# Attention by seven products, followed by a cluster block and an MLP: a ninth score before the first block, the maxima row copied one unit earlier, and x brought back by adding DMA transfers

## The chip, the cores and the metric

The kernel runs on one core of one Trainium2 chip. The metric is the device time of the kernel in microseconds (us), a median over several runs. All data are float32.

Names used below: PE is TensorE (matmuls; PEld its weight loads), DVE is VectorE, ACT is ScalarE, POOL is GpSimd, SP is SyncE, which here only issues DMAs. Each engine has its own queue of instructions and works through it in order.

## The reference

Two layers are applied to x of shape (4, 256, 64, 64), that is, four images of 256 channels and N = 4096 pixels. The first is full self-attention over the pixels:

```python
q = jnp.einsum('oc,bcn->bno', wq, xf) + bq          # 32 channels
k = jnp.einsum('oc,bcn->bon', wk, xf) + bk[None, :, None]
attn = jax.nn.softmax(jnp.einsum('bnd,bdm->bnm', q, k), axis=-1)   # 4096 x 4096
v = jnp.einsum('oc,bcn->bon', wv, xf) + bv[None, :, None]
out = jnp.einsum('bcn,bmn->bcm', v, attn).reshape(B, C, H, W)
return gamma[0] * out + x
```

The second is a block of three parts. A group norm over the whole image, then a clustering of the pixels (features and values by 1x1 convolutions, 4 heads of 24 channels, centres from average pooling, every pixel given to the most similar centre), a projection, and a residual:

```python
y = x + ls1[...] * cluster(group_norm(x, gn1_w, gn1_b), f_w, f_b, v_w, v_b, proj_w, proj_b, sim_alpha, sim_beta)
hdn = conv1x1(group_norm(y, gn2_w, gn2_b), mlp_w1, mlp_b1)      # 256 -> 1024
hdn = conv1x1(jax.nn.gelu(hdn), mlp_w2, mlp_b2)                 # 1024 -> 256
y = y + ls2[...] * hdn
z = jax.nn.relu(batch_norm(y * dw_w[...], dw_g, dw_b, dw_m, dw_v))
z = jax.nn.relu(batch_norm(conv1x1(z, pw_w), pw_g, pw_b, pw_m, pw_v))
```

The first group norm needs mean and variance of the attention's result over all channels and pixels of an image, so nothing of the cluster block can start before the last pixel of the attention is done.

## The kernel before, in words

The four images are worked on one after the other: attention, cluster, MLP. The beginning of the next image's attention (projections, and its first eight scores) is put between the instructions of the cluster and the MLP of the image before it. For image 0 a prologue, `alone`, does it.

**Units.** The attention of an image is a loop of 64 units: 8 blocks `nb` of 512 query pixels, by 8 groups `g` of 512 key pixels. A unit u = 8 nb + g has an SBUF slot of 128 x 2048 numbers (`slots[u]`), in which its scores, then their exponentials lie. There are 12 slots, two of them in the space of the MLP's weights.

**Scores.** A score is made in two halves (`half`). A half is two matmuls into a PSUM tile `sc` (L409), a copy to the slot by ACT (`kept`, L422), and a maximum against the block's running maximum `top` by DVE (L434; L437 for the first of a block, which compares the second half in PSUM with the copied first half). The tile pool `ps_s` has two PSUM buffers; the loop keeps one of them all the time as `hold`, so all scores use the other one, and the next half's matmuls wait for the maximum of the half before.

**Maximum of a query.** After the last score of a block, `fold` and `highest` reduce `top` over partitions to a row of 512 maxima. The row goes through DRAM and comes back spread over all partitions in SBUF (`mr`), and `known` (L531, ACT) copies it into `hold` in PSUM. `highest` is a generator of three steps: a transpose and a reduction on DVE, four small copies on ACT, a reduction, a transpose and the two DMAs. For block 0 the row is made on chip (`across`, `spread`).

**Exponentials.** `exps(u)` subtracts the row from the slot in two DVE instructions (L547), then ACT takes three exponentials (L550, L551, L554) or, in the plain unit g=7, two (L553, L554). `factors(u)` forms with one DVE instruction (L577) and four on POOL (L557) the sums that the seven-product scheme multiplies, and adds to the sum of the exponentials `acc`.

**Weighting.** `weigh(u, av, part)` multiplies values and exponentials in four parts. Units g=0 to 6 use seven products in place of eight on 2 x 2 quarters (28 matmuls, L640), unit g=7 the plain form (18 matmuls, L618).

**Order of a unit.** The order is written out by hand in the loop of `weighting`: the score halves of part 0; `gather` and `known` at g=7; `clear`, which takes the seven-product sums out of PSUM; `exps(u+1)`; maxima; work for the block before; weigh part 0; score halves of part 1; weigh part 1; halves of part 2; `factors(u+1)`; weigh part 2; halves of part 3; weigh part 3; then `tail(u)`. Which half of which score p goes where is set by the table `at`, made by `due_at`: in quarters of a unit, score p (counted from the first that is left to the loop) is due at (14i+10)/5 and (14i+17)/5 for images 1 to 3, at 3i+2 and (6i+7)/2 for image 0; a second bound keeps a score at most LEAD = 11 units ahead, and from p=16 on no earlier than unit 6.

**End of a block.** `clear` and `complete` (L680, DVE) turn the products in PSUM into the attention's numerator `t`; `total` makes the row of denominators, `leave` multiplies by their reciprocals (POOL), `sent` writes the block to DRAM (`att`).

**x comes back.** The group norm's statistics need gamma x attention + x + bias. In the last ten units `load(i)` reads x again from DRAM in four tiles of 1024 pixels (SP's queue), `back(i)` reads the attention of three of them (`tb`, 1 MB each, SP's queue), and `add(i)` puts both and the bias `gbv` together on DVE (L726). The last tile's two blocks are added from SBUF by `add_one` (L726 too). `seen(nb)` (bn_stats, L743) and `pooled(nb)` (L748) take the statistics of a block on DVE.

**At the ends.** `derived` computes constants from the parameters: two square roots on ACT (L193; square root and exponential need different tables in ACT), small DVE instructions and three transposes or matmuls for a weight. It is called as `early` at the end of unit 1 of image 0. At the end of an MLP the next image's `first`, `exps(0)` and `factors(0)` stand ahead of the last pointwise part (`last`).

Of the kernel before, what the change touches and what calls it, by code (L numbers as in the profile page):

```python
# [8 lines left out]
F32 = mybir.dt.float32  # L9
# [5 lines left out]
P = 128  # L15
B, C, H, W = 4, 256, 64, 64
N = H * W
KC = C // P
# [35 lines left out]
def attention_then_cluster_block(  # L54
# [167 lines left out]

    def derived():

        for s, e, g, v, m, b_ in (
            (dw_d, dw_e, "dw_g", "dw_v", "dw_m", "dw_b"),
            (pw_s, pw_e, "pw_g", "pw_v", "pw_m", "pw_b"),
        ):
            rsqrt(s, par(v), BN_EPS)
# [12 lines left out]
        tps = ps_s.tile([P, 2, NB], F32, tag="s", name="wf_p")[:, 0]  # L242
# [5 lines left out]
        nc.vector.tensor_copy(wf_t, tps[:ED, :C])  # L248
        nc.vector.tensor_copy(fvb[:, :ED], tps[:, C : C + ED])
# [43 lines left out]
    def attention(b, xs, ys):  # L293
# [129 lines left out]

        def half(u, h):
# [8 lines left out]
            if g:  # L433
                return lambda: nc.vector.tensor_tensor(top, sc, top, ALU.max)  # L434
            if h:
                first = slots[u][:, PAIR[0]].rearrange("p h r n -> p r h n")
                return lambda: nc.vector.tensor_tensor(tiles(top), tiles(sc), first, ALU.max)  # L437
# [121 lines left out]
        def factors(u):  # L559
# [8 lines left out]
            if g >= SEVEN:  # L568
                if g == SEVEN:
                    plus(both, both, one, ALU.subtract)  # L570
                for acc, q in ((both, B11), (one, B12), (both, B21), (one, B22)):
                    plus(acc, acc, s[:, q])
# [82 lines left out]
        def clear(nb, av):  # L655
# [9 lines left out]
            plus(t[:, 1], t[:, 1], t[:, 0], ALU.subtract)  # L665
            plus(t[:, 3], t[:, 1], t[:, 3], ALU.subtract)
            plus(t[:, 1], t[:, 1], t[:, 2])
            plus(t[:, 2], t[:, 2], t[:, 3])
# [50 lines left out]

        def back(i):  # L720

            t = own["back", i] = spool.tile([P, KC, XT], F32, tag="s", name=f"tb_{b}_{i}")
            nc.sync.dma_start(out=t, in_=own["t"][i].rearrange("p k b n -> p k (b n)"))

        def join(y, t, k):
            nc.vector.scalar_tensor_tensor(y, y, gbv[:, k : k + 1], t, ALU.add, ALU.add)  # L726

        def add(i):

            t = own.pop(("back", i))  # L730
            for k in range(KC):
                join(ys[i][:, k], t[:, k], k)

        def add_one(nb):

            t = ts.pop(nb)
            for k in range(KC):
                y = block(ys, k, nb).rearrange("p (h n) -> p h n", h=2)
                join(y, rows_of(t, k), k)
# [18 lines left out]
        def alone():  # L758
# [13 lines left out]
            for u in range(GRP):  # L772
# [7 lines left out]
                if u % 2 and 4 + u // 2 < SEVEN:  # L780
                    for f in sums(4 + u // 2):
                        f()
                if u == 3:
                    load_rest()
            fold(0)
# [1157 lines left out]
```

## Time and profile before

| | us |
|---|---|
| median of 3 runs | 3443.86 (3443.59 to 3446.1) |
| profiled execution | 3447.51 |
| its span | 3445.7 |
| weighting loop of image 0 | 82.6 to 612.5 |
| image 1 | 938.8 to 1458.6 |
| image 2 | 1785.4 to 2305.1 |
| image 3 | 2607.6 to 3126.3 |
| one matmul of 128x512, mean (L409) | 0.478 |
| copy of a half (L422) | 1.010 |
| maximum of a half (L434) | 1.221 |

The profile is of one execution; a row of the groups gives line, engine, operation, output<-input with the shape, count, then the busy time of all and the mean in ns of one, then the idle time of the engine just before them and what ended it. A row of the waits gives the waiting instruction, what released it, the total, the number of times and the longest. A row of the timeline gives start and duration, and in brackets the idle time before it and its releaser. A row of the stretches gives busy time (and number of instructions) of PE, PEld, DVE, ACT and POOL between two times, the granted clock of PE, and the share and rate of DMA.

### The profile page before, as it was taken

To read this page: it belongs to the slowest core of one execution; us is meant where nothing else is said; L and a number is where in the kernel's file an instruction comes from. 1 tells how busy PE (TensorE), PEld (TensorE's weight loads), DVE (VectorE), ACT (ScalarE), POOL (GpSimd) and SP (SyncE) were. 2 spreads that over 40 slices of the span, in tenths; PEclk is the share of its full clock that TensorE was granted. 3 is DMA by queue.
4 is the path that set the end of the run, shared out by engine and by line. 5 is a ranking of instruction groups with operands and counts; after the bars stand their busy time and mean duration, and the time that the engine had idled before them with its cause. 6 is when DMAs were issued, how large, how long until landed. Compare 5 with 4: busy or idle time off the path is not lost.

```text
span 3445.7 us, 40484 instructions
## 1 busy us (share of the span) xinstructions
PE 3145.7 (91%) x13866; PEld 2484.0 (72%) x13866; DVE 2519.6 (73%) x3666; ACT 1713.1 (50%) x2706; POOL 2234.8 (65%) x2150
## 2 busy tenths in 40 slices
PE   6799998899979999799988999989997899988999
PEld 4577776688657777578866777767875677766687
DVE  4688887677668788766766888776776788876675
ACT  3456562445545655244554555524454565634444
POOL 3467777368447878737835777854763778774664
PEclk8899999999999999899999999989999999999999
DMA  4111214100111111410011111231011111130000
GB/s 152 34 49 56 62 50 154 65 25 28 47 37 59 58 57 53 161 59 19 28 43 37 60 57 59 92 115 59 19 41 39 56 56 62 50 133 1 13 19 25
DMA packets 104062, 197.20 MB, mean 57 GB/s; under 512 B 14672, under 2 KB 29616, under 8 KB 102320
## 3 DMA queue, kind: packets, MB, share of 16 engines
q1 hardware_dynamic: 102896, 193.50, 17.4%
q8 instruction: 110, 1.80, 0.2%
q10 hardware_dynamic: 832, 1.11, 0.1%
q14 instruction: 96, 0.79, 0.1%
q0 software_dynamic: 128, 0.00, 0.0%
HBM read 148.32 MB, written 46.25 MB: 56 GB/s over the span
## 4 chain that ended last, share of the span: by engine, by line
PE 49%; DVE 19%; POOL 15%; issue 9%; ACT 8%; DMA 0%; SPq 0%; ACTq 0%; POOLq 0%; DVEq 0%
PE av L640 10%; PE mo L1559 9%; POOL acc L557 7%; DVE s L547 5%; PE hq L1642 5%; DVE top L434 4%; PE sc L409 4%; DVE t L577 4%; POOL t L557 4%; PE hp L1642 3%; POOL s L557 3%; PE hr L1642 3%; PE fv L1137 3%; PE vp L366 3%; PE av L618 2%
## 5 line engine op out<-in xcount | busy, mean ns | idle before, releaser
L422 ACT COPY s<-sc 128x1024 f32<-128x1024 f32 x512 | 514.0, 1010 | 581.7 <-PE sc L409 567.6
L557 POOL TENSOR_TENSOR s<-t,s 128x512 f32<-128x512 f32 x224 | 285.8, 1276 | 612.8 <-DVE t L577 546.6
L547 DVE TENSOR_TENSOR s<-s,hold 128x1024 f32<-128x1024 f32 x512 | 599.6, 1212 | 71.1 <-ACT hold L531 68.8
L434 DVE TENSOR_TENSOR top<-sc,top 128x1024 f32<-128x1024 f32 x392 | 478.5, 1221 | 155.9 <-ACT s L422 153.0
L409 PE MATMUL sc<-q,k 128*128 128x512 f32 x1024 | 401.0, 478 | 154.9 <-DVE top L434 99.1
L640 PE MATMUL av<-t,v 128*128 128x256 f32 x1792 | 484.1, 394 | 26.8 <-DVE t L680 19.2
L640 PE MATMUL av<-s,v 128*128 128x256 f32 x1792 | 474.8, 388 | 32.2 <-ACT s L551 25.7
L640 PE MATMUL av<-s,sum 128*128 128x256 f32 x1792 | 473.4, 388 | 0.0
L557 POOL TENSOR_TENSOR acc<-acc,t 128x512 f32<-128x512 f32 x352 | 459.2, 1323 | 0.0
L577 DVE TENSOR_TENSOR t<-s,hold 128x1024 f32<-128x1024 f32 x224 | 273.1, 1219 | 198.9 <-ACT s L554 116.3
L640 PEld LDWEIGHTS av<-s,v 128*128 128x128 f32 x1792 | 348.1, 195 | 96.3 <-ACT s L551 29.1
L640 PEld LDWEIGHTS av<-t,v 128*128 128x128 f32 x1792 | 352.2, 198 | 87.0 <-issue 20.7
L1597 ACT ACTIVATE hs<-hs,pv_s 128x256 f32<-128x256 f32 x496 | 232.4, 503 | 344.4 <-DVE hs L1633 344.4
L640 PEld LDWEIGHTS av<-s,sum 128*128 128x128 f32 x1792 | 349.3, 195 | 57.7
L1559 PE MATMUL mo<-hs,w 128*128 128x256 f32 x1512 | 385.3, 381 | 0.4 <-ACT hs L1597 0.4
L409 PEld LDWEIGHTS sc<-q,k 128*128 128x128 f32 x1024 | 177.7, 194 | 265.9 <-DVE top L434 113.4
L557 POOL TENSOR_TENSOR t<-s 128x512 f32<-128x512 f32 x224 | 302.9, 1352 | 34.4 <-PE av L640 16.2
L550 ACT ACTIVATE hold<-s 128x512 f32<-128x512 f32 x224 | 134.8, 602 | 376.6 <-DVE s L547 376.6
L1559 PEld LDWEIGHTS mo<-hs,w 128*128 128x128 f32 x1512 | 283.1, 190 | 47.6 <-ACT hs L1597 6.9
L554 ACT ACTIVATE s<-s 128x1024 f32<-128x1024 f32 x256 | 266.9, 1043 | 0.8
L1633 DVE TENSOR_TENSOR hs<-hq,hs 128x256 f32<-128x256 f32 x496 | 198.6, 421 | 79.6 <-PE hq L1642 69.3
L618 PE MATMUL av<-s,v 128*128 128x512 f32 (+1 forms) x576 | 232.0, 549 | 6.2 <-ACT s L553 6.2
(288 smaller groups left out, 5220.1 us busy)
## 6 DMA issues: line engine op xcount, KB each, us to landing
k<-k SPq DMA_DIRECT2D x256, 256.0 KB, 2.7
x<-in_x SPq DMA_DIRECT2D x62, 512.0 KB, 5.7
out<-xn SPq DMA_DIRECT2D x62, 256.0 KB, 2.1
att<-t SPq DMA_DIRECT2D x48, 256.0 KB, 3.8
tb<-att SPq DMA_DIRECT2D x12, 1024.0 KB, 7.1
q<-q SPq DMA_DIRECT2D x32, 256.0 KB, 4.1
w<-in_w SPq DMA_DIRECT2D x8, 1024.0 KB, 7.8
mr<-row_mx SPq DMA_DIRECT2D x28, 256.0 KB, 3.3
```

The source lines that it names most:

```text
L409: nc.tensor.matmul(sc[:, r, :], k_s[:, (2 * h + r) * P : (2 * h + r + 1) * P], qs[u // GRP], start=True, stop=True,)
L422: nc.scalar.copy(slots[u][:, PAIR[h]].rearrange("p h r n -> p r h n"), tiles(sc))
L434: return lambda: nc.vector.tensor_tensor(top, sc, top, ALU.max)
L547: nc.vector.tensor_tensor(sh, sh, mb.to_broadcast([P, 2, 2, QW]), ALU.subtract)
L554: nc.scalar.activation(s[:, PAIR[1]], s[:, PAIR[1]], AF.Exp)
L557: nc.gpsimd.tensor_tensor(out, x, y, op)
L577: nc.vector.tensor_tensor(t31[u], s[:, B11 : B22 + 1 : 2], b12.to_broadcast([P, 2, 2, QW]), ALU.add)
L618: nc.tensor.matmul(av[2 + c].rearrange("p (h n) -> p h n", h=2)[:, h], own["v"][:, RG * g + t, c * P : (c + 1) * P], s[:, PAIR[t // 2], t ...
L640: nc.tensor.matmul(av[bank][:, half_ * QW : (half_ + 1) * QW], a[:, r], t[:, r], start=(g == 0 and r == 0 and i in (1, 7, 2, 4)), stop=(g ...
L1559: return nc.tensor.matmul(bank[:, half * HB : (half + 1) * HB], a[:, j], t, start=start, stop=stop)
L1597: nc.scalar.activation(src, src, AF.Gelu_apprx_tanh, bias=pvc("b1", P, j + 4 * (i > 1)))
L1642: nc.tensor.matmul(out, w, x, start=True, stop=True)
```

## The change

The change has six parts.

1. The two square roots of `derived` become `roots`, called in the prologue at u=6; the transposes become `wf`, also in the prologue, with a tile of another PSUM pool and copies by ACT. The rest of `derived` is called within unit 0.
2. The ninth score (unit 8) is done ahead of the loop also for images 1 to 3: its first half at the end of the MLP before `exps(0)`, its second after the last pointwise part, `factors(0)` after it.
3. The table of due times is another one, the same for all images: score p, counted from 9, is due at 7i//2 and (14i+7)//4 quarters; LEAD is the only other bound.
4. The first maximum of a block is taken from the two copies in SBUF, not from PSUM. It is held back and issued with the next maximum or at the end of g=5 (`held`, `opened`). For blocks after the first, `known` moves from the start of g=7 to after weigh part 1 of g=6. The second step of `highest` moves from the start of the unit to after `factors`.
5. x is loaded as before, ACT adds the bias (`shift`), and the attention is added to it in SBUF by a DMA with `accum_op=ALU.add` on POOL's queue (`back`, three times, and `back_one` for block 6). `seen` and `pooled` move into the units, one block each.
6. In the last block `clear`, and half of the last sum of exponentials, move from POOL to DVE, and `complete(nb, av, 0)` is called after weigh part 1 of g=7.

```diff
+    def roots():
+        for s, v in ((dw_d, "dw_v"), (pw_s, "pw_v")):
+            rsqrt(s, par(v), BN_EPS)
+        table(AF.Exp)
+
     def derived():
...
-            rsqrt(s, par(v), BN_EPS)
...
-        tps = ps_s.tile([P, 2, NB], F32, tag="s", name="wf_p")[:, 0]
+    def wf():
+
+        tps = ps_m.tile([P, NB], F32, tag="m", name="wf_p")
...
-        nc.vector.tensor_copy(wf_t, tps[:ED, :C])
-        nc.vector.tensor_copy(fvb[:, :ED], tps[:, C : C + ED])
+        nc.scalar.copy(wf_t, tps[:ED, :C])
+        nc.scalar.copy(fvb[:, :ED], tps[:, C : C + ED])
...
+        held = []
+
+        def opened():
+            while held:
+                held.pop()()
...
             if g:
-                return lambda: nc.vector.tensor_tensor(top, sc, top, ALU.max)
+
+                def against():
+                    opened()
+                    nc.vector.tensor_tensor(top, sc, top, ALU.max)
+
+                return against
             if h:
-                first = slots[u][:, PAIR[0]].rearrange("p h r n -> p r h n")
-                return lambda: nc.vector.tensor_tensor(tiles(top), tiles(sc), first, ALU.max)
+
+                a, z = (slots[u][:, q].rearrange("p h r n -> p r h n") for q in PAIR)
+                held.append(lambda: nc.vector.tensor_tensor(tiles(top), a, z, ALU.max))
...
                 for acc, q in ((both, B11), (one, B12), (both, B21), (one, B22)):
-                    plus(acc, acc, s[:, q])
+                    eng = nc.vector if acc is one and nb == NBLK - 1 else nc.gpsimd
+                    eng.tensor_tensor(acc, acc, s[:, q], ALU.add)
...
+        def shift(i):
+            for k in range(KC):
+                nc.scalar.activation(
+                    ys[i][:, k], ys[i][:, k], AF.Identity, bias=gbv[:, k : k + 1]
+                )
+
         def back(i):
 
-            t = own["back", i] = spool.tile([P, KC, XT], F32, tag="s", name=f"tb_{b}_{i}")
-            nc.sync.dma_start(out=t, in_=own["t"][i].rearrange("p k b n -> p k (b n)"))
-
-        def join(y, t, k):
-            nc.vector.scalar_tensor_tensor(y, y, gbv[:, k : k + 1], t, ALU.add, ALU.add)
...
+            nc.gpsimd.dma_start(
+                out=ys[i], in_=own["t"][i].rearrange("p k b n -> p k (b n)"), accum_op=ALU.add
+            )
+
+        def back_one(nb):
+            nc.gpsimd.dma_start(
+                out=block_all(nb), in_=own["t"][nb // 2][:, :, nb % 2], accum_op=ALU.add
+            )
...
+                if u == 6:
+                    roots()
             fold(0)
+            for g in range(4, SEVEN):
+                for f in sums(g):
+                    f()
             dgs["dg"] = across(0)
+            half(GRP, 0)
             spread(0, dgs["dg"])
+            wf()
+            half(GRP, 1)
             exps(0)
             factors(0)
-            score(GRP)
...
-        for p in range(GRP + (b == 0), units):
-            i = p - GRP - (b == 0)
-            q = ((14 * i + 10) // 5, (14 * i + 17) // 5) if b else (3 * i + 2, (6 * i + 7) // 2)
+        for p in range(GRP + 1, units):
+            i = p - GRP - 1
+            q = (7 * i // 2, (14 * i + 7) // 4)
             for h in range(2):
-                at_least = max(RG * (p - LEAD), RG * 6 if p >= 2 * GRP else 0) + 2 * h
-                due_at(*divmod(max(q[h], at_least), RG), p, h)
+                due_at(*divmod(max(q[h], RG * (p - LEAD) + 2 * h), RG), p, h)
...
+            views = {units - 8 + i: i for i in range(6)} | {units - 1: 6}
+
             def tail(u):
...
-                    (units - 11, lambda: (load(0), back(0))),
-                    (units - 10, lambda: load(1)),
-                    (units - 9, lambda: (add(0), back(1), load(2))),
-                    (units - 8, lambda: (seen(0), pooled(0), seen(1), load(3))),
-                    (units - 7, lambda: (pooled(1), add(1), back(2))),
-                    (units - 6, lambda: (seen(2), pooled(2))),
-                    (units - 5, lambda: (seen(3), pooled(3), add(2), next_x(), next_x())),
-                    (units - 4, lambda: (seen(4), pooled(4), load_mix(b), next_x())),
+                    (units - 11, lambda: load(0)),
+                    (units - 10, lambda: (load(1), shift(0), back(0))),
+                    (units - 9, lambda: (load(2), shift(1), back(1))),
+                    (units - 8, lambda: (load(3), shift(2), back(2))),
+                    (units - 7, lambda: shift(3)),
+                    (units - 5, lambda: (next_x(), next_x())),
+                    (units - 4, lambda: (load_mix(b), next_x())),
                     (units - 4, lambda: b == B - 1 and load_mlp(b)),
-                    (units - 3, lambda: (seen(5), pooled(5), add_one(6), next_x(), begin())),
-                    (units - 2, lambda: (seen(6), pooled(6), b < B - 1 and load_mlp(b))),
+                    (units - 3, lambda: (next_x(), begin())),
+                    (units - 2, lambda: (back_one(6), b < B - 1 and load_mlp(b))),
...
-                    if more:
+                    if more and nb == 0:
                         known(mb)
                 if g == SEVEN:
-                    clear(nb, av)
+                    clear(nb, av, nc.gpsimd if more else nc.vector)
...
                     peak = highest(nb + 1)
                     next(peak)
-                    next(peak)
+                if u == 0:
+                    early()
+                if u in views:
+                    seen(views[u])
                 weigh(u, av, 0)
                 for f in due(u, 1):
                     f()
                 weigh(u, av, 1)
+                if g == GRP - 1 and not more:
+                    complete(nb, av, 0)
+                if more and nb and g == GRP - 2:
+                    known(mb)
                 maxima = due(u, 2)
                 if g + 1 < GRP or more:
                     factors(u + 1)
                 if ripe:
+                    next(peak)
                     mb = next(peak)
                 for f in maxima:
                     f()
+                if u in views:
+                    pooled(views[u])
                 weigh(u, av, 2)
                 for f in due(u, 3):
                     f()
+                if g == 5:
+                    opened()
...
-                elif nb and g == 5 and nb < NBLK - 1:
+                elif nb and g == 5:
                     sent(nb - 1)
                 weigh(u, av, 3)
-                if u == 1:
-                    early()
...
-                if g == GRP - 1:
+                if g == GRP - 1 and more:
                     complete(nb, av, 0)
...
         finish(blocks - 1, acc)
-        if nxt:
-            nxt.exps(0)
-            nxt.factors(0)
-        last(blocks - 1, False, nc.vector)
...
+        if nxt:
+            nxt.half(GRP, 0)
+            nxt.exps(0)
+        last(blocks - 1, bool(nxt), nc.vector)
+        if nxt:
+            nxt.half(GRP, 1)
+            nxt.factors(0)
```

## The prediction

> **What bounds the kernel now.** I read the page's head and groups first, then the waits, then the weighting loop by stretches and unit by unit.
>
> ```profile
> span 3445.7 us, 40484 instructions
> PE 3145.7 (91%) x13866; PEld 2484.0 (72%) x13866; DVE 2519.6 (73%) x3666; ACT 1713.1 (50%) x2706; POOL 2234.8 (65%) x2150
> L434 DVE TENSOR_TENSOR top<-sc,top 128x1024 f32<-128x1024 f32 x392 | 478.5, 1221 | 155.9 <-ACT s L422 153.0
> L409 PE MATMUL sc<-q,k 128*128 128x512 f32 x1024 | 401.0, 478 | 154.9 <-DVE top L434 99.1
> ```
>
> PE is nearly always at work, and what it still waits for is mostly one thing: the single free PSUM buffer of the scores. A half score is L409, then the ACT copy L422 (1.01 us), then the DVE maximum L434 (1.22 us), and only then may the next L409 start: about 3.3 us per half at best (3.09 from start to start at 954.46 and 957.55). The waits name who gives the buffer back, and one more cause:
>
> ```profile
> PEld sc L409 <- DVE top L434: 113.4, 205, 4.8
> DVE s L547 <- ACT hold L531: 68.8, 27, 3.7
> PE sc L409 <- DVE top L437: 32.0, 27, 4.9
> ```
>
> Then stretches of one image's loop: a steady block, a first block, two last blocks (columns: PE, PEld, DVE, ACT, POOL busy; granted clock; DMA).
>
> ```profile
> 286.00:346.00 60.00, 57.32 (x246) 46.01 (x246) 49.76 (x53) 35.77 (x50) 47.08 (x40) 1.00 0.18 58
> 930.00:1010.00 80.00, 62.40 (x239) 47.97 (x238) 49.66 (x45) 36.91 (x47) 37.67 (x31) 0.91 0.13 40
> 1391.00:1466.00 75.00, 58.74 (x217) 44.52 (x218) 54.32 (x59) 18.51 (x29) 49.27 (x39) 0.86 0.40 135
> 545.00:620.00 75.00, 59.13 (x213) 44.92 (x214) 54.20 (x58) 18.34 (x29) 49.14 (x39) 0.85 0.40 135
> ```
>
> Cut at each unit's first L640 or L618 matmul, an image's eight blocks take (image 1) 89.9, 60.5, 60.1, 60.0, 60.0, 60.3, 53.5, 75.5 us; image 0 differs only in block 0, 100.9. A steady block's units are 7.0 each, but 8.08 at g=5 (wait for L437) and 9.88 at g=7. Without these two losses (1.1 and 2.1) it would be 56.8, so a steady block holds 3.2 us to win. Blocks 0 and 7 hold far more.
>
> Block 0: why a first block is slow, from the timeline of image 1.
>
> ```profile
> 957.41 2.34 DVE L547 TENSOR_TENSOR s<-s,hold 128x1024 f32<-128x1024 f32 x2
> 957.55 0.72 PE L409 MATMUL sc<-q,k 128*128 128x512 f32 x2
> ...
> 962.87 1.22 DVE L434 TENSOR_TENSOR top<-sc,top 128x1024 f32<-128x1024 f32 x1 [3.12 <-ACT s L422]
> ...
> 964.15 1.22 PE L409 MATMUL sc<-q,k 128*128 128x512 f32 x2 [4.15 <-DVE top L434]
> 964.75 1.61 PEld L640 LDWEIGHTS av<-s,sum 128*128 128x128 f32 x4
> ```
>
> A half at 957.55 meets the exponentials: ACT waits for L547, then runs L550, L551, L554, and only then copies the half (961.85). The next half starts 6.6 us after this one, PE stands 4.15 us, and its four weight loads then take 1.61 us where 0.84 is usual.
>
> Block 7: DVE is the bound there. Start of the block, and its end:
>
> ```profile
> 1387.28 3.81 DVE L726 SCALAR_TENSOR_TENSOR x<-x,gbv,tb 128x1024 f32<-128x1024 f32 x2
> ...
> 1394.29 2.04 PE L640 MATMUL av<-t,v 128*128 128x256 f32 x4 [4.81 <-DVE t L680]
> ...
> 1461.19 1.53 DVE L680 SCALAR_TENSOR_TENSOR t<-av,pv_s,t 128x512 f32<-128x512 f32 x3 [7.41 <-POOL t L557]
> ```
>
> **What the Trainium skill says.** "SBUF — State Buffer", Who interferes with whom: a DVE instruction with two SBUF inputs contends with a GpSimd instruction that reads SBUF. The trace agrees: L726 (x and tb in SBUF) takes 1.9 us for 1024 elements where L434, with one input in PSUM, takes 1.22. "TensorE: Matmul & The Clock Gate", Part 1: an idle window of some 3.4 us halves the clock until the array was busy as long again; the weight loads after the 4.15 us stall agree. "DMA: Bandwidth & Descriptors", SWDGE vs HWDGE vs iDMA: only GpSimd can issue an accumulating DMA. No run here shows one.
>
> **The change, part by part.**
>
> *Derived constants, once.* Image 0's block 0 is 11.2 us longer than the others' 89.7, with two halves fewer (20 against 22), each worth 0.8 us of L409: 12.8 us. This is `derived`: two table loads of 1.28 us on ACT and PE stalls of 2.50 and 4.25. After, its roots run in the prologue at u=6, its transposes in front of the loop, and only some 12 tiny DVE instructions stay (0.2 to 0.3 us each by rows like L281, so 3 us, beside which DVE waits for ACT anyhow). I take -11.5 in the block and +1.5 in the prologue, where the tables and roots (3 us of ACT) now delay the copies of units 6 and 7: -10, between -13 and -6.
>
> *Ninth score before block 0.* Two halves go to the end of the MLP, where PE waits (3.2 and 4.1 us there), and PE is given less to do in block 0: 1.3 us off at the MLP's end (three images), 0.5 in image 0: -4.4.
>
> *Due table in blocks 0 and 1.* Scores come every 3.5 parts (0.875 unit) instead of 2.8. Block 0 has 19 halves instead of 22 (20 in image 0), block 1 17 instead of 16. Ideal PE time of a block is 7x6.04+6.9=49.2 plus 0.78 per half: block 0 before 66.4, measured 89.9, so 23.5 or 1.07 per half is lost to shifted halves like the one shown. At the same loss 19 halves give 84.3; I take 85, since the maxima row of block 1, asked for in g=6, now also comes later: -5. Block 1 was free of this, its halves at fixed parts (0 and 2) of each unit: 60.5. The new table leaves it shifted until unit 13: parts 0,2,3 | 1,3 | 1,2 | 0,2. 49.2+17x(0.78+1.07)=80.7 at full loss, 62.5 at none; five of its eight units are shifted, so 75: +14.5. Sum +9.5 per image, between -5 and +20.
>
> *First maximum from the copies, row copied at g=6.* `held` frees PSUM after the ACT copy, so the 1.1 us at g=5 goes; `known` before g=7 takes away 2.1 where the row is there. Against that: the held maximum is a DVE instruction of 1024 with two SBUF inputs (1.22 to 1.9 us by L434 and L726), queued at the end of g=5 ahead of the exponentials of g=6's unit; I follow it through L547, L550, L551 to a PE wait of some 1.7. And the row starts about 1 us later, as its partition copies move behind weigh part 1, so the early copy L531 can stand in ACT ahead of the copy of a half (0.8). -3.2+1.7+0.8+0.7 for what a late row leaves: 0 per steady block, between -2.5 and +1.5, times 20 blocks.
>
> *x by adding DMA.* It takes the 24 L726 of tb (44.6 us) and half of the 16 small ones off DVE. In block 7 DVE's cycle per unit was L547 2.34, the wait for ACT's three exponentials 2.28, L577 1.22: 5.84; besides it stood adds, bn_stats (1.28 per pair) and pooled (1.2). After, `seen` comes inside the 2.28 and costs nothing (if x landed; else DVE, and L577 behind it, waits, and POOL and PE after them), and `pooled` follows L577: 7.04 per unit, seven of them 49.3, about PE's own 49.2. With 3 for the first unit (ACT's shift(0), two of 1.04, may stand there for x and delay unit 56's exponentials, but the 4.81 goes), 5 for the last seen behind its DMA, and 2.5 for `complete` and sums: 60 against 75.5, -15.5. The DMA on POOL: 0.5 us of issue (bqk_s) to 2; landing between the 5.2 to 6.1 of POOL's tiny ones and 10 (tb's longest, 1 MB); I take 7. POOL's queue also waits for each shift, and behind it stand POOL's sums for the next unit (5.3 us of 7, so 1.7 spare). End of image: the 7.41 wait falls away as `clear` goes to DVE (about 3 us) and a half of the last sum too (1.3 to 2), but seen(6), waiting for back_one(6), now stands in DVE ahead of complete and the reciprocal: +0.5, between -4 and +5. Sum -15, between -20 and -6.
>
> **Sum.** Per image +9.5+0-15=-5.5, by four -22; with -10 and -4.4: -36.4. The profiled execution took 3447.5 (its span and 1.8 around it), so 3411.1; it lay 3.65 above the median 3443.86. Same offset: 3407.5, say 3408.
>
> **Rivals.** *All goes well:* block 1 at 62.5 and block 0 at 80 are 17.5 less than the 160 assumed, -70 over four images: 3338, the steady blocks untouched. With 1.5 of the 3.2 won in 20 blocks it would be 3308, but I don't count on both: 3338. For it: ACT and DVE have slack (36 and 50 of 60). Against it: the 6.6 us pattern follows wherever part 3 meets the exponentials. *It cancels:* the steady blocks lose 1.5 (+30): 3438, and with a late seen(6) 3444; no change. *Slower:* the shifted halves in blocks 0 and 1. Each meeting of a half with the exponentials costs some 3 us, 6.7 where PE stalls past 3.4 us and the clock falls (as 964.15). Blocks 0 and 1 hold about nine such places; at 5.5 instead of the 3.5 assumed they cost 18 more per image: 3480. It decides from 9.1 more per image (36.4 by 4), that is, when the two blocks together pass 169 us. *The DMA doesn't free DVE:* if seen waits 5 us per transfer, block 7 stays near 75, and the whole ends at 3470; the small DMA's 6 us against 14 us of lead (shift at u=54, seen at 56) speaks against it.
>
> **How the numbers follow.** Forecast case (3375 to 3437) 0.38; goes well 0.24; cancels (within 0.2%, which is 6.9 us, about what this measurement can tell from no change) 0.13; slower by blocks 0 and 1 0.19, by the DMA 0.06. So faster 0.62, same 0.13, slower 0.25. The range takes in most of the good and of the slow case and leaves some one in ten on each side: 3335 to 3475. The likeliest case's own range is 3375 to 3437.
>
> **What would show it.** Block 7 at 57 to 63 us, no tb rows, block 0 of image 0 equal to the others; block 0 near 85 and block 1 near 75 with L409 waits on L434 of over 4 us; g=5 at 7.0. Wrong if: block 1 stays at 61 (shifted halves are harmless), steady blocks at 57 or over 62, bn_stats preceded by waits for DMA, or POOL idle behind its DMA issues.

## The result and the profile after

The changed kernel takes 3430.31 us (median of 5 runs, 3422.31 to 3433.43), the kernel before 3446.10 beside it (5 runs). The ratio is 0.9952, with an interval from 0.9938 to 0.9967: some 16 us faster. The forecast was 3408, 36.4 us below the 3443.86 on which it was built. The profiled execution took 3433.43 us.

The head of the page and two groups, columns as before:

```profile
span 3431.7 us, 40532 instructions
PE 3146.0 (92%) x13866; PEld 2480.9 (72%) x13866; DVE 2499.9 (73%) x3656; ACT 1744.4 (51%) x2741; POOL 2229.2 (65%) x2142
L449 DVE TENSOR_TENSOR top<-sc,top 128x1024 f32<-128x1024 f32 x392 | 478.7, 1221 | 197.6 <-ACT s L428 193.4
L415 PE MATMUL sc<-q,k 128*128 128x512 f32 x1024 | 411.3, 488 | 170.7 <-DVE top L449 152.8
```

The wait for the scores' PSUM buffer has not become less; it has moved. The waits:

```profile
PEld sc L415 <- DVE top L449: 194.8, 261, 4.6
PE sc L415 <- DVE top L449: 152.8, 84, 8.4
DVE s L565 <- ACT hold L549: 34.9, 8, 5.6
DVE st L769 <- DMA x<-att: 23.3, 8, 3.7
```

The wait of DVE for the row in `hold` fell from 68.8 to 34.9 us (8 times instead of 27), and the 32.0 us of PE behind the first maximum (L437) are gone. But PE now waits 152.8 us for the later maxima instead of 99.1, with one of 8.4, and a new wait stands there: bn_stats for the adding DMA.

Four stretches of image 1: block 0, block 1, block 3 and block 7 (columns: PE, PEld, DVE, ACT, POOL busy; clock; DMA). Below them, block 7 of the kernel before, from its first weighting matmul to the end of the loop:

```profile
933.20:1020.30 87.10, 66.06 (x251) 50.55 (x250) 50.10 (x46) 37.85 (x49) 48.80 (x41) 0.88 0.12 37
1020.30:1095.00 74.70, 62.39 (x252) 48.76 (x251) 53.67 (x55) 36.40 (x51) 45.61 (x39) 0.95 0.17 50
1153.40:1212.50 59.10, 57.54 (x247) 45.98 (x246) 50.30 (x52) 35.62 (x50) 47.95 (x40) 1.00 0.20 59
1386.50:1445.50 59.00, 53.07 (x216) 41.11 (x216) 46.79 (x52) 25.43 (x35) 47.49 (x41) 0.97 0.72 199
```

```profile
1383.11:1458.62 75.51, 59.11 (x219) 44.57 (x221) 56.31 (x57) 18.03 (x28) 53.92 (x41) 0.89 0.46 159
```

Block 7 lost DVE work (46.8 us of busy time where 56.3 stood) and 16 us of length, and block 1 became 14 us longer. The units, cut at the same places in both traces, give the account. All numbers are us, after minus before, images 0 to 3:

| stretch | image 0 | 1 | 2 | 3 | sum | forecast |
|---|---|---|---|---|---|---|
| start of the loop (prologue) | +3.1 | | | | +3.1 | +1.5 |
| block 0 | -9.5 | -2.8 | -1.1 | -3.4 | -16.8 | -31.5 |
| block 1 | +14.7 | +14.1 | +12.0 | +14.3 | +55.1 | +58 |
| blocks 2 to 5 | -4.1 | -4.5 | -2.8 | -4.2 | -15.6 | 0 |
| block 6 | +2.5 | +2.3 | +2.1 | +3.0 | +9.9 | 0 |
| block 7 | -16.2 | -16.6 | -16.0 | -16.2 | -65.0 | -62 |
| end of the loop to the product with the reciprocals | +2.8 | +4.1 | +4.3 | +3.0 | +14.2 | +2 |
| the rest up to the next loop, or the end | +1.0 | +1.0 | -1.5 | +0.3 | +0.8 | -4.4 |

The sum is -14.3 with rounding; the spans differ by 14.0. The start of the loop, and it alone, is uncertain by some microseconds: seven runs below that leave the prologue as in the changed kernel (e1_table to e5_ninth, e7_known, e9_first) start the loop between 82.2 and 87.0.

Block 1 shows the pattern that the prediction took from block 0 of before, to the hundredth:

```profile
1058.44 0.72 PE L415 MATMUL sc<-q,k 128*128 128x512 f32 x2
...
1063.76 1.22 DVE L449 TENSOR_TENSOR top<-sc,top 128x1024 f32<-128x1024 f32 x1 [3.12 <-ACT s L428]
...
1065.04 1.22 PE L415 MATMUL sc<-q,k 128*128 128x512 f32 x2 [4.15 <-DVE top L449]
```

And the end of image 1's loop, which ended at 1445.50:

```profile
1443.58 1.09 POOL L752 DMA_DIRECT2D x<-att  x1
...
1450.06 1.29 DVE L769 BATCH_NORM_STATS2 st<-x 128x6 f32<-128x512 f32 x2 [3.48 <-DMA x<-att]
...
1453.83 0.95 DVE L963 RECIPROCAL rec<-den 128x128 f32<-128x128 f32 x1
```

The reciprocal starts 8.3 us after the loop, where it was 4.0 before: DVE has waited 3.48 us for the last adding DMA in front of it. In the program this DMA stands at the end of unit 62, which ended at 1438.5, but POOL's queue came to it only at 1443.58, behind sums of exponentials; it landed 6.5 us later.

### The profile page after: what moved, and what is told of

It is laid out like the page before. It is cut to its first block, busy times and chain, and to the rows that moved or that the text cites. A ratio compares the mean times of both kernels' runs of the same rounds, so it can differ in the third digit from the quotient of the medians.

```text
span 3431.7 us, 40532 instructions
## 1 busy us (share of the span) xinstructions
PE 3146.0 (92%) x13866; PEld 2480.9 (72%) x13866; DVE 2499.9 (73%) x3656; ACT 1744.4 (51%) x2741; POOL 2229.2 (65%) x2142
## 4 chain that ended last, share of the span: by engine, by line
PE 40%; POOL 25%; DVE 17%; issue 8%; ACT 8%; DMA 3%; SPq 0%; POOLq 0%; ACTq 0%; DVEq 0%
PE mo L1599 9%; POOL acc L575 8%; DVE s L565 5%; DVE top L449 5%; PE hq L1682 5%; POOL t L575 5%; PE av L659 4%; POOL s L575 4%; POOL acc L591 3%; DVE t L596 3%; PE hp L1682 3%; PE hr L1682 3%; PE sc L415 3%; PE vp L372 3%; PE fv L1177 3%
## 5 line engine op out<-in xcount | busy, mean ns | idle before, releaser
L565 DVE TENSOR_TENSOR s<-s,hold 128x1024 f32<-128x1024 f32 x512 | 599.6, 1212 | 37.1 <-ACT hold L549 34.9
L415 PE MATMUL sc<-q,k 128*128 128x512 f32 x1024 | 411.3, 488 | 170.7 <-DVE top L449 152.8
L659 PE MATMUL av<-t,v 128*128 128x256 f32 x1792 | 474.1, 388 | 23.8 <-DVE t L596 22.6
L659 PE MATMUL av<-s,v 128*128 128x256 f32 x1792 | 467.3, 384 | 6.6 <-ACT s L569 6.4
L575 POOL TENSOR_TENSOR acc<-acc,t 128x512 f32<-128x512 f32 x352 | 445.8, 1286 | 0.0
L659 PEld LDWEIGHTS av<-t,v 128*128 128x128 f32 x1792 | 345.8, 194 | 84.2 <-DVE t L596 33.1
L659 PEld LDWEIGHTS av<-s,v 128*128 128x128 f32 x1792 | 343.7, 192 | 66.3 <-ACT s L569 10.2
## 6 DMA issues: line engine op xcount, KB each, us to landing
x<-att POOLq DMA_DIRECT2D x12, 1024.0 KB, 10.2
```

What stands on the lines that cost most here:

```text
L415: nc.tensor.matmul(sc[:, r, :], k_s[:, (2 * h + r) * P : (2 * h + r + 1) * P], qs[u // GRP], start=True, stop=True,)
L565: nc.vector.tensor_tensor(sh, sh, mb.to_broadcast([P, 2, 2, QW]), ALU.subtract)
L575: nc.gpsimd.tensor_tensor(out, x, y, op)
L659: nc.tensor.matmul(av[bank][:, half_ * QW : (half_ + 1) * QW], a[:, r], t[:, r], start=(g == 0 and r == 0 and i in (1, 7, 2, 4)), stop=(g ...
```

## The experiments

Medians are given with their own runs of the kernel before beside them (3447 to 3448 us), ratios against that. Differences to the changed kernel are taken from 3430.3; its own runs of the kernel before read 3446.1, so that 1 to 2 us of such a difference mean nothing. A cut of a diff leaves lines out where it has three dots. Times of blocks and units are those of the profiled executions.

### The due table

```diff
-            i = p - GRP - 1
-            q = (7 * i // 2, (14 * i + 7) // 4)
+            i = p - GRP - (b == 0)
+            q = ((14 * i + 10) // 5, (14 * i + 17) // 5) if b else (3 * i + 2, (6 * i + 7) // 2)
             for h in range(2):
-                due_at(*divmod(max(q[h], RG * (p - LEAD) + 2 * h), RG), p, h)
+                at_least = max(RG * (p - LEAD), RG * 6 if p >= 2 * GRP else 0) + 2 * h
+                due_at(*divmod(max(q[h], at_least), RG), p, h)
```

> The changed kernel with the due table of before put back (for score 9 on), all else as changed. Theory (shifted halves are what makes block 1 slow): block 1 falls from 74.7 us to 60 or 61, block 0 of images 1 to 3 has one half more and stays at 85 to 90, the steady blocks stay at 59; four images together 50 to 60 us less than the changed kernel, about 3375. Rival (the held first maximum and the earlier copy of the row make block 1 slow, not the table): block 1 stays above 70 and the time stays within 10 us of 3430.

Measured: 3365.91 us, ratio 0.9765 (0.9751 to 0.978), 64 us less than the changed kernel. Block 1 takes 58.3 to 58.8 us, its stretch of image 1 below, and block 0 stays at 86 to 89 (image 0: 92.9). The rival falls: the held maximum and the early row are all in this kernel, and block 1 is as quick as the blocks after it. (It has 16 halves here and 17 in the changed kernel; one half is 0.8 us of PE.)

```profile
999.80:1058.60 58.80, 57.46 (x248) 46.02 (x247) 50.01 (x52) 35.61 (x50) 44.65 (x37) 1.00 0.19 59
```

Block 1 accounts for 62 of the 69 us between the two profiled spans. Another 8.7 come from a place that no theory had named, the start of the loop of images 1 to 3, 2.9 us each. (Image 0's loop starts 3.5 us earlier too, but all of that lies ahead of the sixth score of the prologue, where nothing was changed.) First the changed kernel, then this one:

```profile
932.65 0.73 PE L415 MATMUL sc<-q,k 128*128 128x512 f32 x2 [2.17 <-ACT s L428]
933.21 1.02 PE L659 MATMUL av<-s,v 128*128 128x256 f32 x4
```

```profile
911.58 1.02 PE L415 MATMUL sc<-q,k 128*128 128x512 f32 x2
912.44 1.02 PE L659 MATMUL av<-s,v 128*128 128x256 f32 x4
```

The new table puts the first half of score 9 into part 0 of unit 0, in PE's queue ahead of the first weighting matmul. It waits there for the copy of the ninth score's second half, which frees the PSUM buffer. From the first exponentials to the first weighting matmul it takes 7.33 us in the changed kernel (before: 7.42, 7.43 and 8.33), and 4.42 here. So the ninth score does save 3 us per image, and the new table gave them back.

Inside block 0 the table moved more than the total shows. In images 1 to 3 of the changed kernel, units 0 to 6 take 66.9 to 69.5 us and unit 7 18.7 to 19.4; with the table of before it is 73.3 to 76.6 and 12.6 to 13.0.

### The ninth score

From e1_table on, undone as well, so that the table is wholly that of before:

```diff
-        for p in range(GRP + 1, units):
+        for p in range(GRP + (b == 0), units):
...
+        if nxt:
+            nxt.exps(0)
+            nxt.factors(0)
+        last(blocks - 1, False, nc.vector)
...
-        if nxt:
-            nxt.half(GRP, 0)
-            nxt.exps(0)
-        last(blocks - 1, bool(nxt), nc.vector)
-        if nxt:
-            nxt.half(GRP, 1)
-            nxt.factors(0)
```

> The kernel e1_table with the ninth score undone as well for images 1 to 3: exponentials and factors of unit 0 stand ahead of the last pointwise part again, and both halves of score 8 come in unit 0 (so the due table is wholly that of before). Theory as in the prediction (the two halves fill waits of PE at the MLP's end): the stretch from the first exponentials to the loop is 1.3 us longer than in e1_table and block 0 takes 2 to 4 us more; 10 to 15 us more over three images. Rival (the wait at the MLP's end is hidden anyway, since the halves wait there for the hold tile, the copy and the pointwise part): the stretch is the same, 7.3 to 7.4 us, and only block 0 moves, by 2 to 3 us: 6 to 9 us in all. Second rival: no difference, within 4 us.

Measured: 3376.17 us, ratio 0.9794 (0.9779 to 0.9808), 10.3 more than e1_table. From the first exponentials to the loop it takes 7.43, 7.42 and 8.33 us, as before the change: 3.0, 3.0 and 3.9 more, 9.9 together. Block 0 of images 1 to 3 moved by +1.8, -2.6 and -0.2. The theory has the right place with two to three times the size; that block 0 is shorter without these two halves was not seen.

### The statistics behind the last adding DMA

```diff
-            views = {units - 8 + i: i for i in range(6)} | {units - 1: 6}
+            views = {units - 8 + i: i for i in range(6)}
...
             nc.scalar.copy(rdens[nb], inv)
+            seen(6)
+            pooled(6)
```

> The changed kernel with the statistics of block 6 (bn_stats and pooled) moved from unit 63 to behind the copy of the reciprocals, after the loop. Theory (in the changed kernel bn_stats waits for the last adding DMA in front of the reciprocal): the reciprocal starts 4 us after the loop's end instead of 8.4, and each image gains 3 to 4 us, 12 to 16 in all. Rival (the longer end comes from clear and the last sum on DVE): the reciprocal still starts 7 us or more after the loop, gain under 4 us in all.

Measured: 3406.82 us, ratio 0.9887 (0.987 to 0.9903), 23.5 less. The reciprocal starts 2.65 us after the loop (image 3: 6.1), and the product with the reciprocals follows at 7.3 to 7.8 (image 3: 11.1), where the changed kernel had 12.4 to 12.8 and 14.7. That is 5.1, 4.7, 5.6 and 3.6 us, 19 of the gain; the rest is scattered and was not traced. The timeline of DVE in image 1:

```profile
1441.08 0.95 DVE L963 RECIPROCAL rec<-den 128x128 f32<-128x128 f32 x1
1443.93 1.28 DVE L769 BATCH_NORM_STATS2 st<-x 128x6 f32<-128x512 f32 x2 [1.90 <-DMA x<-att]
```

bn_stats still waits for the DMA, but now while DVE would wait for ACT's copy anyway. The rival falls: `clear` and the last sum stay on DVE. The gain is larger than expected: the end is now shorter than before the change (8.5 to 9.6, image 3: 11.8), so the DMA's wait was more than the whole of the loss there.

### What brings x back

`back` fills `tb` on SP's queue again, and `add(2)` and `add_one(6)` come back too:

```diff
-                    (units - 11, lambda: load(0)),
-                    (units - 10, lambda: (load(1), shift(0), back(0))),
-                    (units - 9, lambda: (load(2), shift(1), back(1))),
-                    (units - 8, lambda: (load(3), shift(2), back(2))),
-                    (units - 7, lambda: shift(3)),
...
+                    (units - 11, lambda: (load(0), back(0))),
+                    (units - 10, lambda: load(1)),
+                    (units - 9, lambda: (add(0), back(1), load(2))),
+                    (units - 8, lambda: load(3)),
+                    (units - 7, lambda: (add(1), back(2))),
...
```

> The changed kernel with x brought back as before: tb by SP's queue, both added with the bias on DVE, in the units where before had them; the statistics stay spread as changed. Theory (taking the adds off DVE is what shortens block 7): block 7 goes from 59.3 back to 69 to 75, block 6 to 53.5; the end of the image is 3 to 4 us shorter, since no DMA stands before the last statistics; in all 20 to 45 us more than the changed kernel. Rival (spreading the statistics into DVE's waits is enough): block 7 stays under 63, and the kernel is as fast as the changed one or 15 us faster.

Measured: 3443.60 us, ratio 0.9987 (0.998 to 0.9993), 13 more, where the theory had 20 to 45. Its adds on DVE, from its groups, and its stretch of block 7 of image 1:

```profile
L751 DVE SCALAR_TENSOR_TENSOR x<-x,gbv,tb 128x1024 f32<-128x1024 f32 x24 | 44.0, 1870 | 0.0
```

```profile
1385.90:1454.60 68.70, 55.94 (x219) 42.96 (x221) 59.52 (x60) 18.04 (x28) 52.29 (x39) 0.93 0.50 173
```

Block 7 takes 68.7 to 69.8 us, block 6 53.9 to 54.3. So of the 16 us that block 7 lost, 6 are won by the other edits together (the spread statistics, `clear`, the early `complete`, which were not taken apart), 10 by the adding DMA. Against these 10 the DMA costs 1.5 to 2.2 in block 6, and at the end of the image 3.5 to 6.7 (the product with the reciprocals comes 5.7 to 7.6 us after the loop here, 11.2 in image 3). Net it is worth 3 us per image as it was placed.

### The row and unit 7 of block 0

Unit 7 of block 0 went from 12.5 us to between 18.7 and 19.4 (image 0: from 14.9 to 18.7). Two edits, each alone on the changed kernel. First the row's second step back in its place for block 0, then the maximum of part 0 ahead of the exponentials:

```diff
                     next(peak)
+                    if nb == 0:
+                        next(peak)
...
                 if ripe:
-                    next(peak)
+                    if nb:
+                        next(peak)
```

> The changed kernel with the second step of the maxima row back in its old place for block 0 only. Theory (unit 7 of block 0 takes 18.7 us because the row for block 1 lands late): unit 7 falls by 2 to 4 us, 8 to 16 us over four images. Rival (unit 7 is long because the held maximum stands between the exponentials and the maximum that frees PSUM): under 1 us per image.

```diff
+                if u == GRP - 1:
+                    while maxima:
+                        maxima.pop(0)()
                 if g + 1 < GRP or more:
                     exps(u + 1)
```

> The changed kernel with one move: in unit 7 of each image the maximum of the part 0 half goes ahead of the exponentials that wait for the row of block 1, so that it frees PSUM early. Theory (unit 7 of block 0 is 18.7 us long because that maximum stands in DVE behind the wait of 5.4 us for the row and the exponentials, and PE waits 8.3 us for it and goes cold): unit 7 falls to 12 to 15 us, 15 to 25 us over four images. Rival (the row itself sets the end of unit 7, since the weighting of unit 8 needs its exponentials): under 2 us per image, 8 us in all.

Measured: 3421.90 us with the row (ratio 0.9924, 0.9909 to 0.9939), 8 less, which the intervals barely tell from the changed kernel; unit 7 still takes 18.1 to 18.4; what moved is spread over blocks 0 and 1. With the maximum ahead 3407.30 us (0.9886, 0.9872 to 0.9899), 23 less, and unit 7 takes 15.4 to 16.0, not the 12 to 15 of the theory; 11 of the 23 us lie in block 1. This is what happened in the changed kernel:

```profile
1006.45 2.35 DVE L565 TENSOR_TENSOR s<-s,hold 128x1024 f32<-128x1024 f32 x2 [5.41 <-ACT hold L549]
...
1008.72 1.58 DVE L455 TENSOR_TENSOR top<-s 128x1024 f32<-128x1024 f32 x1
...
1010.40 1.23 DVE L449 TENSOR_TENSOR top<-sc,top 128x1024 f32<-128x1024 f32 x1
...
1011.77 1.19 PE L415 MATMUL sc<-q,k 128*128 128x512 f32 x2 [8.26 <-DVE top L449]
```

The maximum that frees PSUM stood in DVE's queue behind the wait for the row, the subtraction, and the held maximum. With it ahead, the longest such wait of PE in this unit is 4.8 to 5.2 us in images 1 to 3, against 8.3 to 8.4.

The late row is not ruled out as the reason for the rest. In the changed kernel the subtraction that needs the row starts 4.8 to 5.0 us into unit 7, in the kernel before 1.9. Putting the second step back brought that only to 3.6 to 4.2. In e1_table, where unit 6 takes 9.7 to 11.3 us instead of 7.0, it is 1.9 to 2.3, and unit 7 12.6 to 13.0 without any new order. So under the new table unit 6 has become too short to cover the way of the row: this follows from the times, and no run changes the row alone.

### The held maximum and the early row

Each undone alone on the changed kernel:

```diff
-                a, z = (slots[u][:, q].rearrange("p h r n -> p r h n") for q in PAIR)
-                held.append(lambda: nc.vector.tensor_tensor(tiles(top), a, z, ALU.max))
+                first = slots[u][:, PAIR[0]].rearrange("p h r n -> p r h n")
+                return lambda: nc.vector.tensor_tensor(tiles(top), tiles(sc), first, ALU.max)
...
-            half(GRP, 1)
+            half(GRP, 1)()
...
```

> The changed kernel with the first maximum of a block taken from PSUM at once, as before, not from the two copies later. Theory (holding it back removes the wait of g=5, 1.1 us, and its late place costs about as much in g=6 and g=0): g=5 goes from 6.97 to 8.1, g=6 from 8.5 to 7.0 or 7.5 and g=0 from 7.86 to 7.0; steady blocks stay within 1 us of 59.1, the time within 15 us. Rival (held is what wins): g=5 rises and g=6 doesn't fall, 1.1 us per block, 20 us in all.

```diff
-                    if more and nb == 0:
+                    if more:
                         known(mb)
...
-                if more and nb and g == GRP - 2:
-                    known(mb)
```

> The changed kernel with the row's copy into PSUM back at the start of unit 7 of every block. Theory (the copy at g=6 is what shortened g=7 from 9.88 to 7.79, and costs little): g=7 returns to 9.5 to 10, g=6 falls from 8.5 to 8 at most, some 1.5 to 2 us per block, 30 to 45 us in all over five or six blocks of four images. Rival (g=7 became short by the held maximum, the copy's place doesn't matter): g=7 stays under 8.3 and the time within 8 us.

Measured without `held`: 3413.10 us, ratio 0.9893 (0.9879 to 0.9908), 17 less. In block 2 g=5 went from 6.97 to 8.45, g=6 from 8.5 to 7.01: the block stays at 58.5. In blocks 3 to 5, where g=0 falls from 7.86 to 7.2 as well, 58.4 to 58.7 us stand in place of 59.1 to 59.8. Holding the maximum back moves a loss from one unit to the next and wins nothing in a steady block, as the theory said, and in three blocks it costs 0.7. In block 0 it costs more: 82.3 to 84.2 us (image 0: 87.4) without it, instead of 85.8 to 88.9 (91.5), 16 us in all, and most of it in unit 7 (15.0 instead of 18.7 to 19.4), where the held maximum stood ahead of the one that frees PSUM. Against this, the loops start 4 us later in image 0 and 1.3 to 1.6 in the others, since the first maximum of the ninth score now stands there.

Measured with the row copied at g=7: 3453.95 us, ratio 1.0018 (1.0011 to 1.0025), 24 more. g=7 is 9.87 again, g=6 unchanged at 8.5, g=0 7.04 instead of 7.86: 1.3 us per block in blocks 3 to 5 (1.9 in block 2), less than expected because of g=0. The early row is the edit that pays in the steady blocks.

### The derived constants

```diff
-                if u == 6:
-                    roots()
...
-            wf()
...
-                if u == 0:
-                    early()
...
+                if u == 1:
+                    early()
...
```

> The changed kernel with the derived constants as before: square roots, tables and the transposes at the end of unit 1 of image 0, nothing of them in the prologue. Theory as in the prediction: 10 us more (block 0 of image 0 11.5 more, the loop starts 1.5 earlier). Rival (the small DVE instructions that stay are what costs, and the shifted halves leave the loop waiting anyway): 2 to 6 us more.

Measured: 3430.15 us, ratio 0.9946 (0.9929 to 0.9962): no difference to the changed kernel. Both expectations fall. Block 0 of image 0 takes 98.8 us instead of 91.5, 7.3 more, but the loop starts at 79.1 instead of 85.7. Of these 6.6 us, 3.7 lie ahead of the sixth score's copy, where both kernels are the same. From that copy on it takes 24.0 us in the changed kernel and 21.1 here (23.8 to 24.5 in the seven runs with the same prologue). So the prologue pays 2.9 us; its trace shows how: the roots and two table loads of 1.28 us hold up ACT from 67.46 to 72.84, of which 1.88 is a wait for DVE, ahead of the last score's copies. By these two numbers the split should still win some 4 us; the medians, which can't tell 2 us, show none, and which other place takes them back is open.

### Versions that beat both

Taken together: the table of images 1 to 3 of before for all images, the first maximum from PSUM, the statistics of block 6 late, the maximum of unit 7 ahead (`c_best`); the same with the constants as before (`c_derived`); and `c_best` with each shift and adding DMA one unit later:

```diff
-            views = {units - 8 + i: i for i in range(6)}
+            views = {units - 7 + i: i for i in range(6)}
...
-                    (units - 10, lambda: (load(1), shift(0), back(0))),
+                    (units - 10, lambda: load(1)),
+                    (units - 9, lambda: (load(2), shift(0), back(0))),
...
```

> The changed kernel with five of its edits taken back or mended together: the due table of images 1 to 3 of before for all images, the first maximum from PSUM as before, the statistics of block 6 behind the copy of the reciprocals, and the maximum of unit 7's part 0 ahead of the exponentials. If the gains of the single runs (64 by the table, 23 by the statistics, 17 by the first maximum) add up: 3310 to 3330. If they are partly the same time (the table and the first maximum both concern block 0): 3330 to 3350. What stays of the change is the adding DMA, the early row, the ninth score and the split of the constants.

> c_best with the derived constants as before (at the end of unit 1 of image 0). Theory (the prologue pays back what block 0 gains): within 4 us of c_best. Rival (with block 0 free of shifted halves the split is worth its 10 us): 6 to 12 us more than c_best.

> c_best with shift and adding DMA one unit later (first in unit 55, statistics of blocks 0 to 5 in units 57 to 62). Theory (in the changed kernel ACT stands 3.6 us in shift(0) for x, ahead of clear and the exponentials of unit 56, which makes the last unit of block 6 8.5 us instead of 6.9): that unit falls to 7, block 7 stays within 1 us, 6 to 10 us less in all. Rival (the next shift stands as badly, before the exponentials of unit 57): no difference, within 3 us.

Measured: c_best 3347.74 us (ratio 0.971, 0.9697 to 0.9724), c_derived 3349.88 (0.9718, 0.9705 to 0.9732), c_late 3337.69 (0.9684, 0.9671 to 0.9697). The last is 110 us faster than the kernel before and 93 faster than the changed one.

c_best lies at the upper end of what was expected: the gains are partly the same time, and one is turned round. With the table of before, block 0 of images 1 and 2 takes 95.2 us against 87.4 and 89.2 in e1_table (image 3: 91.4 against 86.3). In these two images some 6 us of it are unit 0, 13.4 us instead of 7.1. The trace of c_best shows it:

```profile
909.64 1.22 DVE L454 TENSOR_TENSOR top<-sc,s 128x1024 f32<-128x1024 f32 x1 [3.80 <-ACT s L428]
...
912.05 2.07 PE L658 MATMUL av<-t,v 128*128 128x256 f32 x4 [3.70 <-DVE t L595]
```

The first maximum of the ninth score, no longer held, waits in DVE for its copy, ahead of the factors of unit 0. Holding back only this one was not tried. Another 2 us are unit 7, 14.6 instead of 12.6 to 13.0: with the table of before it was short already, and that the maximum ahead helps there is not shown. c_derived says again that the split of the constants is worth nothing that can be told (2 us, the runs of the two overlap): block 0 of image 0 takes 96.6 us instead of 90.2, and the prologue from the sixth score on 23.8 instead of 28.2. The theory of c_late holds, 10 us less: the last unit of block 6 takes 6.87 us, not 8.3 to 8.9, and block 7 57.4 to 57.8 instead of 58.8 to 59.4: shift(0) had stood 3.6 us in ACT, waiting for x, ahead of `clear` and the exponentials of unit 56.

## Why the prediction was right or wrong

The direction was right and the size was not: -36.4 was forecast, -15.8 is what the medians show and -14.0 the profiled spans. By the table above, the missing 22 us are 14.7 in block 0, 12.2 at the end of the image, 9.9 in block 6, 5.2 in the rest up to the next loop and 1.6 in the prologue; blocks 2 to 5 gave back 15.6, blocks 1 and 7 some 3 each.

**Right.** Block 7 at 60 us (59.0 to 59.5), block 1 at 75 (72.7 to 74.8), and the reasons for block 1: the shifted halves are shown by e1_table, and the mechanism (a half that meets the exponentials, 6.6 us from start to start, 4.15 us of waiting) recurs unchanged. For block 7 the prediction named DVE's relief and the spread statistics together; e4_dve splits them, 10 to 6 (the 6 with the other edits).

**The end of the image** is a term with the right mechanism and the wrong size: "seen(6), waiting for back_one(6), now stands in DVE ahead of complete and the reciprocal" was put at +0.5 per image, after 5 in block 7 for the same wait. In block 7 the wait cost nothing: its last unit took 7.03 us, no more than its 18 matmuls. It fell behind the loop instead, where the step had let the gain of `clear` pay for it, and was +3.5 per image, 14.2 against 2. e2_seen6 takes 19 us away in that one place.

**Block 0 and the derived constants.** Half of the miss in block 0 is image 0. There -11.5 was forecast for the constants, with +1.5 in the prologue. e6_derived shows 7.3 and 2.9, c_derived 6.4 and 4.4, and both times no gain in the medians that can be told from 2 us. The step that failed took all by which image 0's block was longer for the work of `derived`, and put the price of the same work in the prologue at half or less of what it was.

**Block 0 of the other images** was forecast at 85 and took 85.8 to 88.9, and that it came so near is in part luck. Two terms were wrong and cancelled. Units 0 to 6 became 7.9 to 9.8 us shorter, where three halves fewer at 1.85 us each were taken for 5.5; unit 7 became 6.2 to 6.9 us longer, where 0.7 stood for a later row. What the order in DVE's queue does there was missing: e9_first takes 3 of the 6 us away, e8_held 4. The late row itself remains a likely reason for the rest, as said above.

**Block 6**, +9.9 against 0: shift(0)'s wait for x was counted once, as 3 us within block 7's first unit, against the 4.81 that left. It falls into the last unit of block 6 and comes on top, 7.0 of the 9.9; c_late takes it away. The other 2.9 are the block's first unit, 7.5 to 7.9 us instead of 7.0, which e8_held brings back to 7.2 or 7.5.

**The ninth score**, -4.4 against -1.2 (the stretch from exponentials to loop: 0.1, 0.1 and 1.0 shorter). Its term was too small, 1.3 where e5_ninth shows 3.0 to 3.9, and the new table took it back: that its first half lands at part 0 of unit 0, in PE's queue ahead of the weights and waiting for a copy, was not looked at. A moved instruction was costed by its busy time and not by what stands behind it.

**The steady blocks**, 0 against -15.6: 0.2 to 1.6 per block, 1.0 on average. The early row (e7_known, 1.3) is better than assumed, `held` a little worse than neutral (e8_held). The losses set against the early row were too high. Without this unforeseen gain the time would have stayed about the same.

## What to carry to other kernels

When the buffer that everything waits for is freed by an instruction in a shared queue, look at what that instruction stands behind: here, putting it ahead of a wait for a row that comes by DMA was worth 23 us, though no work was saved. Two schedules with nearly the same number of pieces differed by 16 us in 75 (block 1, 17 halves and 16) by where the pieces fell, so look at where each piece lands in the unit, and at the first one in particular. A transfer that replaces arithmetic needs its consumer placed where that engine waits anyway, and its issue needs a free place in its queue; here the same adding DMA was worth 3 us or 9 us per image (e4_dve against the changed kernel and against e2_seen6) by where one pair of statistics stood.

## What the runs showed of the hardware

An adding DMA of 1 MB from DRAM to SBUF on POOL's queue lands 10.2 us after its issue (median; 7.9 to 12.1) and takes POOL 0.85 to 0.98 us, where the plain transfer of tb on SP's queue landed in 7.1. One of 512 KB lands in 6.5. From the DMA issues of the changed kernel:

```profile
x<-att POOLq DMA_DIRECT2D x12, 1024.0 KB, 10.2
```

The prediction had taken 7. During block 7 of image 1 the DMA engines are busy for 0.72 of the time at 199 GB/s, against 0.46 and 159 before. The median of the loads of x rose from 5.7 us to 7.7; they are also issued closer together now, so this is not shown to be the adding DMA's doing. The maximum from two SBUF copies takes 1.69 us on average (1.58 at 1008.72), against 1.22 with one input in PSUM, within the 1.2 to 1.9 that were assumed. That the second SBUF input matters when POOL is at work can be read more closely from one instruction of the kernel before, the add of 512 elements (minimum, median and maximum in ns):

```profile
L726 DVE SCALAR_TENSOR_TENSOR x<-x,gbv,t x16: 744/880/1754, 600.4 to 3140.0; 128x512 f32<-128x512 f32 x16
```

It takes 0.75 us in the eight cases where POOL is idle beside it, and 1.01 to 1.75 in the eight where POOL is busy throughout. L434, with one input in PSUM, takes 1.22 in both cases.
